# Side work of a Mamba-style scan kernel shared out by what is left of its unit, with the C·h rounds regrouped as three, two, three

## The chip, the cores and the metric

The kernel runs on one core of one Trainium2 chip. The metric is the device time in microseconds (us) of one execution; the median of several runs counts. A TensorE matmul in this kernel is always float32, and the profile records each such matmul as two weight loads and two passes.

## What is computed

The reference takes 2 sequences of 1024 tokens with 512 features (2048 tokens in all), and computes, cut to what matters:

```python
xn    = x * rsqrt(mean(x*x) + 1e-6) * norm_w
xn    = xn * sigmoid((xn @ select_proj_w.T + select_proj_b) * select_gate)
delta, B, C = split(xn @ x_proj_w.T)              # 128 columns each
delta = softplus(delta @ dt_proj_w.T + dt_proj_b) # 512 columns
h     = exp(delta * A) * h + (delta * xn) * B     # per token; state 512 x 128
y     = sum over the 128 states of C * h
x1    = layernorm(x + (y + x * D_param) @ out_proj_w.T)
out   = layernorm(x1 + (silu(x1 @ w_gate.T) * (x1 @ w_up.T)) @ w_down.T)   # 2048 hidden
```

The scan over tokens is the long part: it has 512 x 128 states for each of 2048 tokens.

## The kernel before

**The main loop.** The scan is cut into stretches of 32 tokens (`st`, 64 of them), each into two halves (`i`), and each half into eight *slots*. There are so 1,024 slots, numbered `k`; `r = k % 8` is a slot's *place* in its half. A slot does the same basic work each time: two matmuls for `bu` (L689, the input term), two matmuls for `a` (L407, the exponent of the decay, for the slot after it), both on 32 of the 128 rows of the array; two `Exp` on ScalarE, which read `a` and write `a_sb` (L414); on VectorE a small add that carries the state over (L708) and one scan over 128 x 1024 elements (L709), which reads `a_sb` and `bu` and writes a part of `h`. `bu` has two PSUM buffers, `a` has two (one for each of its matmuls), `a_sb` has three. A matmul for `a` has to wait until ScalarE has read the buffer that it writes.

**C·h.** Eight rounds of four matmuls (`y_round`, L426) for each half multiply `h` of the half before by C. The list `ROUNDS` says which rounds stand at which place. They are issued after the basic work of the slot.

**Side work.** All else is written as Python generators and shared out over the slots at places 0, 2, 3, 5 and 6: the projections of the next lot of 256 tokens (`pre`: units `ss`, `sel`, `xp`, `b`, `z`, `uT`, `t`), the output projection of a tile of 128 tokens (`post`: `zT`, `op`), and the feed-forward part (`ffn`: `x1T`, eight units `gu` and two units `d` for each tile). A *unit* is a group of matmuls into the one PSUM bank that all the side work shares (`ps_m`, one buffer). A generator yields "P" before a unit, "H" between the *parts* of a unit, and "E" at its end; `Work.tensor()` issues one part of the unit that holds the bank, or begins the next unit. A part is one matmul for `d`, `op`, `sel`, `xp` and `ss`, two matmuls for `gu`, and two transposes for `zT`, `x1T` and `uT`. So `gu` has 8 parts (16 matmuls), `d` has 16 parts (16 matmuls), `op` has 8, `sel` and `xp` have 4. `give_back()` at the start of a slot frees the bank of a unit that has ended; what follows it on the other engines (a copy from PSUM, an add) is issued then.

**How many parts a slot gets.** `PARTS` gives a number for each place, and a credit carries over what could not be used:

```python
credit = min(credit + PARTS[r], 6)
for _ in range(min(credit, 4) if PARTS[r] else 0):
    if not work.tensor():
        break
    credit -= 1
```

**Order.** All engines run their instructions in the order in which Python issues them; nothing reorders them later. Weights of `ffn` come in pieces of 512 KB through five buffers, issued on SyncE's queue (L506), some pieces ahead of their use.

**The end.** After the last slot come the last eight rounds of C·h, then whatever side work is left: always the last tile's `zT`, `op`, first layernorm, `x1T`, `gu`, `d` and last layernorm, and what remains of the tile before it (tile 14 of 0 to 15).

Of the kernel before, what the change touches and what calls it, by code (L numbers as in the profile page):

```python
# [17 lines left out]
TC = 256  # L18


ROUNDS = ((), (0, 1, 2), (), (), (3, 4, 5), (), (), (6, 7))
PARTS = (4, 0, 3, 3, 0, 3, 3, 0)
RMS_EPS = 1e-6
LN_EPS = 1e-5

# [9 lines left out]
def kernel(  # L35
# [25 lines left out]
    NF = wgu_s.shape[0]  # L61
    NM = D // P
# [79 lines left out]
    def col(group, m):  # L142
        return vec[:, group, m : m + 1]
# [10 lines left out]

    made = {}

    def misc(name):
        return bank_pool[0].tile([P, 512], FP, tag="m", name=name)


# [3 lines left out]
    def pre(c):  # L164

        t0, n = lots[c]
        n_j, n_s = n // P, n // S
# [15 lines left out]
        def matmuls(ps, w, m, rhs):  # L183
            for k in range(NM):
                nc.tensor.matmul(  # L185
                    ps[:, 0:n], w[:, k, ts(m, P)], rhs[:, k, :],
                    start=(k == 0), stop=(k == NM - 1),
                )
                yield "H" if k + 1 < NM else "E"
# [7 lines left out]
        for m in range(NM):  # L197
            nc.scalar.activation(xT[:, m, :], xT[:, m, :], AF.Copy, scale=col(V_NORM, m))
        yield "P"
        ps = misc(f"ss_{c}")  # L200
        for k in range(NM):
            nc.tensor.matmul(  # L202
                ps[:, 0:n], ones, u[:, k, :], start=(k == 0), stop=(k == NM - 1)
# [12 lines left out]


        for m in range(NM):
            ps = misc(f"sel_{c}_{m}")
            yield from matmuls(ps, sel_w, m, xn)  # L220
            nc.scalar.activation(
                u[:, m, :], ps[:, 0:n], AF.Relu,
                bias=neg[:, 1, m : m + 1], scale=neg[:, 0, m : m + 1],
            )
            nc.scalar.activation(
                dt[:, m, :], ps[:, 0:n], AF.Abs, bias=gate_b[:, m : m + 1], scale=col(V_GATE, m)
            )
            yield "P" if m + 1 < NM else "E"
# [9 lines left out]
            decay()  # L238

        for g, dst in ((0, low), (2, c_sb)):  # L240
            ps = misc(f"xp_{c}_{g}")
            yield from matmuls(ps, xp_w, g, xn)
            nc.scalar.copy(dst, ps[:, 0:n])
            yield "P"

        ps = misc(f"b_{c}")
        for j in range(n_j):
            for k in range(NM):
                nc.tensor.matmul(  # L249
# [12 lines left out]
        yield "P"  # L262

        for a in range(0, NM, 2):
            ps = misc(f"z_{c}_{a}")
            for m in (a, a + 1):
                nc.tensor.matmul(  # L267
                    ps[:, ts(m - a, n)], dt_w[:, ts(m, P)], low, start=True, stop=True
                )
                yield "H" if m == a else "E"  # L270
            for m in (a, a + 1):
                z = ps[:, ts(m - a, n)]
                nc.scalar.activation(u[:, m, :], z, AF.Relu, bias=col(V_DTB, m))
                nc.scalar.activation(dt[:, m, :], z, AF.Abs, bias=col(V_DTB, m))  # L274
            yield "P" if a == 0 else "E"
# [4 lines left out]

        for j in range(n_j):
            yield "P"
            ps = misc(f"uT_{c}_{j}")
            for m in range(NM):
                nc.tensor.transpose(ps[:, ts(m, P)], u[:, m, ts(j, P)], ident)
                if m == 1:
                    yield "H"
            yield "E"
            t = pre_pool.tile([P, D], FP, tag="row", name=f"uT_{c}_{j}")
            nc.scalar.copy(  # L290
                t.rearrange("p (g m c) -> p m g c", g=4, m=NM),
                ps.rearrange("p (m g c) -> p m g c", m=NM, g=4),
            )
            for st in range(4):
                nc.sync.dma_start(
                    ub_d[t0 // S + 4 * j + st, :, :, 0, :].rearrange("g t q -> t g q"),
                    t[ts(st, S), :].rearrange("t (g q) -> t g q", g=4),
                )
            if c == 0:
                load(0)  # L300
                diag(0, 0)
                diag(0, 1)
        yield "P"
        ps = misc(f"t0_{c}")
        for m in range(NM):
            nc.tensor.matmul(
                ps[0:n_s, ts(m, P)],
# [89 lines left out]
    def place(k):  # L397
        h, r = divmod(k, 8)
        m, pair = divmod(r, 2)
        return h, m, pair  # L400
# [47 lines left out]
    def post(tt):  # L448

        zT = post_pool.tile([P, NM, P], FP, tag="zT", name=f"zT_{tt}")  # L450
        nc.sync.dma_start(zT, x_q.rearrange("(m p) t -> p m t", p=P)[:, :, ts(tt, P)])
        yield "E"
        yield "E"
        nc.gpsimd.tensor_tensor(zT, zT, dq.unsqueeze(2).to_broadcast([P, NM, P]), ALU.mult)
        yield "E"
        yield "P"
        ps = misc(f"zT_{tt}")
        for s in range(4):
            nc.tensor.transpose(ps[:, ts(s, P)], yrs[tt][:, s, :], ident)
            if s == 1:  # L460
                yield "H"
        yield "E"
        z = zT.rearrange("p m (s t) -> p s m t", t=S)
        nc.vector.tensor_tensor(
            z, z, ps.rearrange("p (s m t) -> p s m t", m=NM, t=S), ALU.add
        )
        x1 = post_pool.tile([P, D], FP, tag="x1", name=f"x1_{tt}", bufs=4)
        nc.sync.dma_start(x1, xf[tt])
        yield "P"
        ps = misc(f"op_{tt}")  # L470
        for half in (slice(0, 256), slice(256, 512)):
            for k in range(NM):
                nc.tensor.matmul(  # L473
                    ps[:, half], zT[:, k, :], out_w[:, k, half], start=(k == 0), stop=(k == NM - 1)
                )
                yield "H" if half.start == 0 or k + 1 < NM else "E"
        nc.vector.tensor_tensor(x1, x1, ps, ALU.add)
        yield "E"
        yield from normalize(x1, f"a{tt}")
        work.add(ffn(tt, x1))  # L480
# [12 lines left out]
    def ffn(tt, row):  # L493
# [17 lines left out]
        fetch(4)  # L511
        x1T = ffn_pool.tile([P, NM, P], FP, tag="x1T", name=f"x1T_{tt}")
        yield "P"
        ps = misc(f"x1T_{tt}")
        for m in range(NM):
            nc.tensor.transpose(ps[:, ts(m, P)], row[:, ts(m, P)], ident)
            if m == 1:
# [6 lines left out]
        for f in range(0, NF, 2):  # L524
            fetch(at + 4)
            yield "P"
            ps = misc(f"gu_{tt}_{f}")
            for b in range(2):
                w = pieces[at + b].rearrange("p (a k h) -> p a k h", a=2, k=NM)
                for a in range(2):  # L530
                    for k in range(NM):
                        nc.tensor.matmul(  # L532
                            ps[:, ts(2 * a + b, P)], w[:, a, k, :], x1T[:, k, :],
                            start=(k == 0), stop=(k == NM - 1),
                        )
                        if k % 2:
                            yield "E" if a and b and k + 1 == NM else "H"
            at += 2
            gu = ffn_pool.tile([P, 2, 2 * P], FP, tag="gu", name=f"gu_{tt}_{f}", bufs=2)
            nc.scalar.copy(gu, ps.rearrange("p (a t) -> p a t", a=2))  # L540
            work.add(silu(gu, hid[:, f : f + 2, :], f"{tt}_{f}", ready), front=True)
        while len(ready) < NF // 2:
            yield "E"
        for half in range(2):
            fetch(at + 4)
            yield "P"
            ps = misc(f"d_{tt}_{half}")
            for f in range(NF):
                if f == NH:
                    fetch(at + 6)  # L550
                w = pieces[at + f // 4].rearrange("p (f d) -> p f d", f=4)
                nc.tensor.matmul(  # L552
                    ps[:, 0:HD], hid[:, f, :], w[:, f % 4, :],
                    start=(f == 0), stop=(f == NF - 1),
                )
                yield "H" if f + 1 < NF else "E"
            part_of = row[:, ts(half, HD)]
            nc.vector.tensor_tensor(part_of, part_of, ps[:, 0:HD], ALU.add)
            at += 4
# [38 lines left out]
    class Work:  # L598


        def __init__(self):
            self.gens, self.holder = [], None

        def add(self, gen, front=False):
            item = [gen, next(gen)]
# [23 lines left out]
        def tensor(self):  # L629

            if self.holder is not None:
                if self.holder[1] != "H":
                    return False
                self.step(self.holder)
                return True
            for item in self.gens:
                if item[1] == "P":
                    self.holder = item
                    self.step(item)
                    return True  # L640
            return False

# [5 lines left out]
    work = Work()  # L648
# [13 lines left out]
    for b in range(2):  # L662
        decay_exp(0, b, decay_mm(0, b))

    pres, begun, credit = {}, set(), 0
    for k in range(NG):
        h, m, pair = place(k)
        st, i = divmod(h, 2)
        r = k % 8

        if PARTS[r]:
            work.give_back()
        if r == 0:
            hs[h] = half_pool.tile([P, 256, S], FP, tag="h", name=f"h_{h}")
            if i == 0:
                c = lot_of[st]
# [10 lines left out]
        for b in range(2):  # L687
            g = 2 * pair + b
# [26 lines left out]
        if h:  # L715
            for b in ROUNDS[r]:
                y_round(h - 1, b)
        credit = min(credit + PARTS[r], 6)
        for _ in range(min(credit, 4) if PARTS[r] else 0):
            if not work.tensor():  # L720
                break
            credit -= 1

        j, r4 = divmod(k, 4)
        if r4 == 3:
# [93 lines left out]
```

## Time and profile before

| | |
|---|---|
| median of three runs | 2837.61 us (2833.27 to 2842.39) |
| the profiled execution's own time | 2842.96 us |
| its span, first to last instruction | 2841.2 us |
| first scan begins, last scan ends | 43.2 us, 2760.6 us |
| TensorE busy | 2727.4 us (96%) |
| VectorE busy | 2522.9 us (89%) |
| ScalarE, GpSimd busy | 1549.8 us (55%), 1783.3 us (63%) |
| mean granted TensorE clock | 0.987 |

The profiled execution lies 5.4 us above the median of the runs, and its span is 1.8 us shorter than its own time. A line such as `L689 PE MATMUL bu<-du,ub` in the profile means: the instruction of line 689 of the kernel, on TensorE, that reads `du` and `ub` and writes `bu`. In a timeline the first number is the start in us from the start of the span, the second the duration; `[0.86 <-DVE h L709]` says that the engine sat idle for 0.86 us just before and what ended that. A busy TensorE there is an engine with some matmul under way, not one at its peak rate.

### The profile page before, as it was taken

What the parts mean: (1) busy time and instruction counts of PE and PEld (TensorE: products, weight loads), DVE (VectorE), ACT (ScalarE), POOL (GpSimd) and SP (SyncE); (2) the same over time, 40 slices, a digit from 0 to 9 for tenths busy, and PEclk for the clock granted to TensorE, in tenths of its full rate; (3) what the DMA queues carried; (4) which work ended last, traced back from release to release, by engine and by line L of the source; (5) the groups of instructions that cost most, each with busy time, mean ns of one, the idle gap of its engine ahead of it and who ended that gap; (6) DMA issues with size and microseconds to landing.
All of it is one profiled execution on the core that took longest, in us unless ns stands there. A gap on an engine that the chain in (4) does not pass through costs nothing.

```text
span 2841.2 us, 57463 instructions
## 1 busy us (share of the span) xinstructions
PE 2727.4 (96%) x22728; PEld 1484.1 (52%) x22728; DVE 2522.9 (89%) x2144; ACT 1549.8 (55%) x3105; POOL 1783.3 (63%) x2016
## 2 busy tenths in 40 slices
PE   7879999999999999999999999999999999999998
PEld 4324554555555554555544555555555555555558
DVE  2999898999999999999999999999999999999980
ACT  4546555555565455654656556555555554555442
POOL 4556675666667675775667667667576666657552
PEclk7999999999999999999999999999999999999999
DMA  2012222224223232233312333132331323332336
GB/s 75 16 30 66 86 77 79 87 73 134 86 62 116 86 121 64 83 96 105 123 43 84 105 104 104 57 100 93 112 101 47 113 87 109 101 105 96 107 103 208
DMA packets 112380, 258.67 MB, mean 91 GB/s; under 512 B 11568, under 2 KB 49456, under 8 KB 112112
## 3 DMA queue, kind: packets, MB, share of 16 engines
q1 hardware_dynamic: 112112, 254.99, 27.6%
q8 instruction: 181, 2.97, 0.4%
q14 instruction: 87, 0.71, 0.1%
HBM read 242.23 MB, written 12.71 MB: 90 GB/s over the span
## 4 chain that ended last, share of the span: by engine, by line
PE 75%; DVE 18%; issue 3%; ACT 2%; POOL 1%; DMA 0%; SPq 0%; DVEq 0%; POOLq 0%; ACTq 0%
PE bu L689 28%; PE gu L532 17%; DVE h L709 15%; PE y L426 13%; PE d L552 7%; PE a L407 4%; PE sel L185 2%; PE op L473 1%; PE xp L185 1%; DVE bu L708 1%; ACT a_sb L414 1%; PE b L249 1%; PE ss L202 0%; PE z L267 0%; DMA ub_d<-uT 0%
## 5 line engine op out<-in xcount | busy, mean ns | idle before, releaser
L709 DVE TENSOR_TENSOR_SCAN h<-a_sb,bu 128x1024 f32<-128x1024 f32 x1024 | 2341.2, 2287 | 159.2 <-POOL ddt L378 43.2
L414 ACT ACTIVATE a_sb<-a 128x496 f32<-128x496 f32 x2048 | 1089.0, 585 | 1142.6 <-PE a L407 1013.3
L689 PE MATMUL bu<-du,ub 32*128 32x512 f32 x4096 | 1198.0, 646 | 52.5 <-DVE h L709 28.3
L407 PE MATMUL a<-ddt,a_t 32*128 32x512 f32 x4096 | 1240.7, 646 | 2.8 <-ACT t L313 2.8
L378 POOL TENSOR_TENSOR ddt<-dt,hot 128x512 f32<-128x512 f32 x512 | 534.5, 1050 | 225.2 <-PE a L407 225.1
L532 PEld LDWEIGHTS gu<-x1T,w 128*128 128x128 f32 x4096 | 481.7, 192 | 232.8 <-issue 155.0
L388 POOL TENSOR_TENSOR du<-ub,hot 128x512 f32<-128x512 f32 x512 | 536.4, 1052 | 25.7 <-PE a L407 22.3
L532 PE MATMUL gu<-x1T,w 128*128 128x128 f32 x4096 | 537.3, 283 | 11.2 <-ACT t L313 4.5
L689 PEld LDWEIGHTS bu<-du,ub 32*128 32x128 f32 x4096 | 337.2, 184 | 375.8 <-issue 205.6
L426 PE MATMUL y<-h,cz 128*32 128x256 f32 x8192 | 524.7, 385 | 1.9 <-DVE h L709 1.3
L426 PEld LDWEIGHTS y<-h,cz 128*32 128x32 f32 x8192 | 227.7, 109 | 406.7 <-issue 271.9
L407 PEld LDWEIGHTS a<-ddt,a_t 32*128 32x128 f32 x4096 | 371.5, 184 | 19.9 <-ACT a_sb L414 9.6
L708 DVE TENSOR_TENSOR bu<-bu,cd 128x32 f32<-128x32 f32 x992 | 184.9, 186 | 83.1 <-PE a L407 80.2
L552 PE MATMUL d<-w,hid 128*128 128x256 f32 x1024 | 256.9, 393 | 1.1 <-ACT dt L274 1.1
L552 PEld LDWEIGHTS d<-w,hid 128*128 128x128 f32 x1024 | 183.5, 189 | 121.6 <-issue 92.5
L570 POOL TENSOR_SCALAR gu<-gu 128x256 f32<-128x256 f32 x128 | 108.3, 846 | 209.4 <-ACT gu L540 208.4
L578 POOL TENSOR_TENSOR hid<-gu,e 128x256 f32<-128x256 f32 x128 | 93.1, 728 | 141.7 <-ACT e L576 140.8
L440 POOL TENSOR_TENSOR yc<-yc,pick 128x512 f32<-128x512 f32 x64 | 66.7, 1042 | 168.7 <-ACT yc L439 168.7
L365 POOL TENSOR_TENSOR cd<-cd,h 128x256 f32<-128x256 f32 x124 | 106.5, 859 | 44.5 <-DVE h L709 44.5
L571 POOL TENSOR_TENSOR gu<-gu 128x256 f32<-128x256 f32 x128 | 93.4, 730 | 10.7
L540 ACT COPY gu<-gu 128x512 f32<-128x512 f32 x128 | 75.3, 588 | 33.5 <-PE gu L532 33.3
L323 POOL TENSOR_TENSOR dt<-dt,u 128x512 f32<-128x512 f32 (+1 forms) x36 | 41.3, 1151 | 68.7 <-ACT dt L320 68.7
(86 smaller groups left out, 1252.6 us busy)
## 6 DMA issues: line engine op xcount, KB each, us to landing
w<-in_wgu_s_dram SPq DMA_DIRECT2D x256, 512.0 KB, 3.8
w<-in_wd_s_dram SPq DMA_DIRECT2D x128, 512.0 KB, 4.0
cd<-dt_d SPq DMA_DIRECT2D x62, 256.0 KB, 4.0
ub<-ub_d SPq DMA_DIRECT2D x64, 128.0 KB, 2.0
ub_d<-bt SPq DMA_DIRECT2D x64, 64.0 KB, 1.8
ub_d<-uT SPq DMA_DIRECT2D x64, 64.0 KB, 1.8
zT<-in_x_q_dram SPq DMA_DIRECT2D x16, 256.0 KB, 4.0
x<-in_x_dram SPq DMA_DIRECT2D x16, 256.0 KB, 3.6
```

The source lines that it names most:

```text
L365: nc.gpsimd.tensor_tensor(cd, cd, last, ALU.mult)
L378: nc.gpsimd.tensor_tensor(ddts[j][:, m, :, :], made[lot_of[st]][0][:, a + m, toks(st)].unsqueeze(1).to_broadcast([P, 16, S]), hot[:, ts(i, ...
L388: nc.gpsimd.tensor_tensor(dus[j][:, m, :, :], uv[:, a + m, :].unsqueeze(2).to_broadcast([P, 16, S]), hot.unsqueeze(1).to_broadcast([P, 16, ...
L407: nc.tensor.matmul(ps, a_t[ts(g, 32), m, :], ddts[k // 4][ts(g, 32), m % 2, :, :], start=True, stop=True,)
L414: nc.scalar.activation(a_sb[:, k % 3, ts(b, 16), 1:], ps[:, :, 1:], AF.Exp, scale=-1.0)
L426: nc.tensor.matmul(ys[st][ts(m, 32), ts(i, 256)], cz[st % 3][:, at : at + 32], hs[h][:, ts(m, 64), ts(b, 4)], start=(i == 0 and b == 0), s ...
L532: nc.tensor.matmul(ps[:, ts(2 * a + b, P)], w[:, a, k, :], x1T[:, k, :], start=(k == 0), stop=(k == NM - 1),)
L552: nc.tensor.matmul(ps[:, 0:HD], hid[:, f, :], w[:, f % 4, :], start=(f == 0), stop=(f == NF - 1),)
L570: nc.gpsimd.tensor_scalar_max(g, g, -80.0)
L689: nc.tensor.matmul(bu[:, ts(b, 16), :], prepared[st][ts(g, 32), 1, :], dus[k // 4][ts(g, 32), m % 2, :, :], start=True, stop=True,)
L708: nc.vector.tensor_tensor(first, first, left[:, at : at + 2, i, :], ALU.add)
L709: nc.vector.tensor_tensor_scan(hs[h][:, ts(r, 32), :].rearrange("p q t -> p (q t)"), a_sb[:, k % 3, :, :].rearrange("p q t -> p (q t)"), b ...
```

## The change

The rounds of C·h are regrouped: rounds 0 to 2 stay at place 1, rounds 3 and 4 stay at place 4, and rounds 5 to 7 stand at place 7 (before: 3, 4, 5 at place 4 and 6, 7 at place 7). The credit is dropped. Each unit says how many parts it has when it takes the bank (`misc(name, parts)`), and `Work` counts down what is left of it. A slot first issues one part. If three or fewer are left of that unit then, it issues all of them. If more are left, it issues up to as many in all as `PARTS` says, or four if the unit has just begun and the place is 0 or 6. `PARTS` becomes 3, 4, 4, 3, 3 at places 0, 2, 3, 5, 6 (before 4, 3, 3, 3, 3).

```diff
-ROUNDS = ((), (0, 1, 2), (), (), (3, 4, 5), (), (), (6, 7))
-PARTS = (4, 0, 3, 3, 0, 3, 3, 0)
+ROUNDS = ((), (0, 1, 2), (), (), (3, 4), (), (), (5, 6, 7))
+PARTS = (3, 0, 4, 4, 0, 3, 3, 0)
...
-    def misc(name):
+    def misc(name, parts):
+        work.left = parts
         return bank_pool[0].tile([P, 512], FP, tag="m", name=name)
...
-            ps = misc(f"gu_{tt}_{f}")
+            ps = misc(f"gu_{tt}_{f}", 2 * NM)
...
-            ps = misc(f"d_{tt}_{half}")
+            ps = misc(f"d_{tt}_{half}", NF)
...
             if self.holder is not None:
                 if self.holder[1] != "H":
                     return False
+                self.left -= 1
+                self.fresh = False
                 self.step(self.holder)
                 return True
             for item in self.gens:
                 if item[1] == "P":
                     self.holder = item
                     self.step(item)
+                    self.left -= 1
+                    self.fresh = True
                     return True
...
-        credit = min(credit + PARTS[r], 6)
-        for _ in range(min(credit, 4) if PARTS[r] else 0):
-            if not work.tensor():
-                break
-            credit -= 1
+        if PARTS[r] and work.tensor():
+            more = work.left
+            if more > 3:
+                more = (4 if work.fresh and r in (0, 6) else PARTS[r]) - 1
+            for _ in range(more):
+                work.tensor()
```

More of the change, by code (lines that the diff above doesn't have):

```diff
@@ L199, in pre @@
         yield "P"
-        ps = misc(f"ss_{c}")
+        ps = misc(f"ss_{c}", NM)
         for k in range(NM):
@@ L218, in pre @@
         for m in range(NM):
-            ps = misc(f"sel_{c}_{m}")
+            ps = misc(f"sel_{c}_{m}", NM)
             yield from matmuls(ps, sel_w, m, xn)
@@ L240, in pre @@
         for g, dst in ((0, low), (2, c_sb)):
-            ps = misc(f"xp_{c}_{g}")
+            ps = misc(f"xp_{c}_{g}", NM)
             yield from matmuls(ps, xp_w, g, xn)
@@ L244, in pre @@
             yield "P"
-        ps = misc(f"b_{c}")
+        ps = misc(f"b_{c}", n_j)
         for j in range(n_j):
@@ L264, in pre @@
         for a in range(0, NM, 2):
-            ps = misc(f"z_{c}_{a}")
+            ps = misc(f"z_{c}_{a}", 2)
             for m in (a, a + 1):
@@ L282, in pre @@
             yield "P"
-            ps = misc(f"uT_{c}_{j}")
+            ps = misc(f"uT_{c}_{j}", 2)
             for m in range(NM):
@@ L303, in pre @@
         yield "P"
-        ps = misc(f"t0_{c}")
+        ps = misc(f"t0_{c}", 1)
         for m in range(NM):
@@ L456, in post @@
         yield "P"
-        ps = misc(f"zT_{tt}")
+        ps = misc(f"zT_{tt}", 2)
         for s in range(4):
@@ L469, in post @@
         yield "P"
-        ps = misc(f"op_{tt}")
+        ps = misc(f"op_{tt}", 2 * NM)
         for half in (slice(0, 256), slice(256, 512)):
@@ L513, in ffn @@
         yield "P"
-        ps = misc(f"x1T_{tt}")
+        ps = misc(f"x1T_{tt}", 2)
         for m in range(NM):
@@ L601, in __init__ @@
         def __init__(self):
-            self.gens, self.holder = [], None
+            self.gens, self.holder, self.left, self.fresh = [], None, 0, False
         def add(self, gen, front=False):
@@ L663 @@
         decay_exp(0, b, decay_mm(0, b))
-    pres, begun, credit = {}, set(), 0
+    pres, begun = {}, set()
     for k in range(NG):
```

## The prediction

> **What bounds the kernel now.** I read the page's busy times and its chain of work first:
>
> ```profile
> span 2841.2 us, 57463 instructions
> PE 2727.4 (96%) x22728; PEld 1484.1 (52%) x22728; DVE 2522.9 (89%) x2144; ACT 1549.8 (55%) x3105; POOL 1783.3 (63%) x2016
> PE 75%; DVE 18%; issue 3%; ACT 2%; POOL 1%; DMA 0%; SPq 0%; DVEq 0%; POOLq 0%; ACTq 0%
> ```
>
> TensorE carries three quarters of the chain, VectorE most of the rest. VectorE's floor is 2.48 us a slot (scan 2.29, carry add and gaps 0.19), 19.86 us for eight slots. Next, the table of busy time by stretch, over eight slots in which all side work is `gu`:
>
> ```profile
> core 0: us, PE busy (x) PEld busy (x) DVE busy (x) ACT busy (x) POOL busy (x), PEclk, DMA share, GB/s
> 1379.20:1400.10 20.90, 20.90 (x196) 12.15 (x192) 19.49 (x17) 12.27 (x25) 14.75 (x18) 1.00 0.38 127
> ```
>
> TensorE fills all of it, VectorE has a microsecond to spare. So TensorE sets the pace, and what counts is its time slot by slot, from the first `bu` of a slot to that of the next. TensorE's timeline gives it (places 5, 6, 7, and an empty place 0):
>
> ```profile
> 2333.27 0.69 PE L689 MATMUL bu<-du,ub 32*128 32x512 f32 x1
> ...
> 2334.34 0.71 PE L532 MATMUL gu<-x1T,w 128*128 128x128 f32 x4
> 2334.98 0.69 PE L689 MATMUL bu<-du,ub 32*128 32x512 f32 x1
> ...
> 2335.58 0.71 PE L407 MATMUL a<-ddt,a_t 32*128 32x512 f32 x2
> ...
> 2336.63 1.07 PE L426 MATMUL y<-h,cz 128*32 128x256 f32 x16
> 2337.63 0.69 PE L689 MATMUL bu<-du,ub 32*128 32x512 f32 x1
> ...
> 2339.64 0.69 PE L689 MATMUL bu<-du,ub 32*128 32x512 f32 x1 [0.86 <-DVE h L709]
> ```
>
> The slot with one part of `gu` takes 1.71 us. The next slot has two rounds of C·h, which elsewhere make 2.07 us (1383.53 to 1385.60), and takes 2.65: its second `a` starts 0.6 us after its first `bu`, since ScalarE still reads the `a` of the slot before. A short slot saves nothing below some 2.3 us. The empty slot at 2337.63 lasts 2.01 although its work is 0.97; there VectorE is the later one.
>
> Reading all 1,023 slots so, at full clock: 12 matmuls of y 2.51, 8 of y 2.07 (0.108 each); 8, 6, 4, 2 matmuls of `gu` 3.05, 2.60, 2.16, 1.71 (0.223 each); 4, 3, 1 of `d`, `op`, `sel` or `xp` 3.00, 2.56, 1.70 (0.432 each); four transposes 1.66; empty 0.97. Any side work thus costs 0.30 beyond its matmuls (3.05 - 8 x 0.223 - 0.97). These sum to 2516 us, the slots took 2717: 201 us are waits. The waits of short slots, read as the excess of the pair of slots, are steady: y8 0.23, gu4 0.13, gu2 0.58, one matmul 0.59, transposes 0.63, an isolated empty slot 1.3 to 1.6.
>
> The end, TensorE's timeline:
>
> ```profile
> 2760.70 3.64 PE L426 MATMUL y<-h,cz 128*32 128x256 f32 x58 [1.26 <-DVE h L709]
> ...
> 2767.31 0.33 PE L459 MATMUL zT<-ident,yr 128*128 128x128 f32 x1 [2.01 <-POOL yr L442]
> 2769.03 5.41 PE L473 MATMUL op<-out_w,zT 128*128 128x256 f32 x16 [1.39 <-DVE zT L464]
> 2774.27 13.98 PE L552 MATMUL d<-w,hid 128*128 128x256 f32 x64
> 2788.09 0.60 PE L516 MATMUL x1T<-ident,x 128*128 128x128 f32 x4
> 2790.74 30.48 PE L532 MATMUL gu<-x1T,w 128*128 128x128 f32 x256 [2.06 <-ACT x1T L520]
> ```
>
> All 32 `d` of tile 14 stand between the last tile's `op` and its `x1T`; the layernorm there needs 3.5 of these 14 us (2774.4 to 2777.9).
>
> **The change part by part.** The order of the changed program on TensorE shows what goes where; it does what it says.
>
> *Work moved into the loop.* 20 `d` and 2 `gu` more, 4 y fewer (they follow the last slot's `bu`, under the last scan: nothing): 20 x 0.432 + 2 x 0.223 - 4 x 0.108 = +8.7.
>
> *Fewer slots with side work.* Empty slots go from 44 to 56: 12 x 0.30 = -3.6. Work of the slots: +5.1.
>
> *Split units.* One-part slots (gu2, or one matmul) fall from 49 to 17. Before: 49 x 0.585 = 28.7 of wait. After: the 17 follow a y8 slot, whose 0.23 is part of their 0.59 ("y8, d1" gave 0.59 in all), so 17 x 0.36 = 6.1. That is -22.6. `gu4` goes from 23 to 43: +2.6. Of the empty slots 34 and 35 lie in the first 100, where VectorE sets the pace and they cost nothing; the later ones go from 10 to 21: 11 x 1.45 = +16.0 (ends 1.3 and 1.6: 14.3 to 17.6). Sum -4.0.
>
> *Rounds of C·h.* Round 5 moves from place 4 to 7. y12 and y8 slots stay as many, so 0. It reads `h` of the half before, done eight slots ago. The copy of y at place 0 comes 0.43 later, 2.5 before the next round needs the bank. The scan of the next half, which overwrites `h`, starts 1.55 after the next `bu`, which stands behind the round. If this cover were gone: at most 0.43 for each of 64 stretches, no end of mine.
>
> *Queues.* A `gu` unit now ends at place 3 and its copy (0.59 on ScalarE) is issued at place 5, ahead of that slot's `Exp`; the next unit starts 1.06 after that slot's `bu`, so it is covered. Weight pieces land in 3.8 us and are asked for a unit ahead, 9.7 us now (2 x 3.05 + 2.3 + 1.3). GpSimd's and VectorE's lists are the same work in slightly other places.
>
> *`op` after `zT`.* Its add sits on VectorE behind a scan, and `op` waits for it: 11.3 us over the run, without the stall of the next item. Afterwards 13 tiles have `zT` at place 6 and `op` at 0, two slots later; the nearest row (3 and 5) waits 0.78: 10.1. So -1 (ends -11 and +5).
>
> *One stall.* At 433.4 the slot with the first `op` lasted 4.6 too long, and the clock fell to half until 442.4; its eight slots lost 5.9. It may stay or go: -2 (0 to -5.9).
>
> Loop: 5.1 - 4.0 - 1 - 2 = -1.9.
>
> *The end.* From the last scan's end (2760.64) `gu` starts after 30.1 us. After: y 3.6; 12 `d` 5.2; then VectorE first does tile 14's add and statistics (0.4 + 0.7 + 0.2) and only then `zT`'s add (0.7), so `op` starts at about 11.1; `op` at full clock 3.5; layernorm 3.5; `x1T` 0.6, copy 0.6, gaps 0.4: 19.7. That is -10.4. Ahead of the last tile's weights SyncE's queue now has tile 14's output, which waits for its layernorm to about 12; the first piece lands at 16, needed at 19.7. TensorE is more idle here, and the clock shows what that can do (next rows). I take 2 us for it (0 to 3.5): -8.5.
>
> Sum -10.4: the profiled 2841.2 becomes 2830.8, and the median, 5.4 below that execution's own time, 2837.6 - 10.4 = 2827.
>
> **The clock.** Table by stretch again, same columns:
>
> ```profile
> 220.60:224.00 3.40, 2.61 (x16) 1.24 (x16) 3.19 (x5) 2.12 (x4) 3.40 (x4) 0.99 0.00 0
> 224.00:227.40 3.40, 3.40 (x24) 0.90 (x20) 3.30 (x3) 1.58 (x3) 3.14 (x3) 0.50 0.01 2
> ...
> 2787.40:2790.80 3.40, 1.34 (x9) 0.95 (x8) 1.30 (x3) 1.08 (x4) 0.27 (x1) 1.00 0.66 231
> 2790.80:2794.20 3.40, 3.40 (x16) 3.40 (x17) 0.00 (x0) 0.63 (x1) 0.00 (x0) 0.50 0.38 104
> ```
>
> The granted clock (before the last two columns) is half in stretches of 3.4 us that follow stretches in which TensorE was busy for 0.98 to 2.61 us of 3.4. Each costs up to 1.7 us of TensorE's time. None of the ten empty slots after the first 100 has one beside it.
>
> The Trainium skill ("TensorE: Matmul & The Clock Gate", Part 1) says that the clock halves after at least one idle window of about 3.4 us. No empty slot is idle that long, so by the rule the loop loses nothing and the sum stays at 2827. The rows show a fall after a window busy for three quarters; their case stands below, at 2849.
>
> **The rivals.** *The clock falls in the new empty slots* (slower). Place: place 5 after a y8 slot, 21 empty slots after the first 100. Price 1.7 each. For it: a y8 slot and an empty one hold some 2 us of work in 4.6, as little as the stretches above. Against: none of ten before. From 6 such falls the gain is gone, from 11 it is a loss over 0.3%; all 21 give 2827 + 36 = 2863, the 13 that recur every 64 slots or so 2827 + 22 = 2849, which I take.
>
> *The waits are not saved and the end is late* (no change). If the excess of short slots was VectorE's and only showed on TensorE, the loop gains nothing of the 4.0 + 1 + 2 and costs +5.1; with two more half-clock stretches in the end and weights 1.5 us late its gain is 5.5. Sum about 0: 2837. For it: 18% of the chain is VectorE. Against: its spare microsecond in eight slots.
>
> *More waits go* (faster): 8 of `op`'s 11 us go, as `zT` and `op` now always stand two slots apart, and the whole stall: loop 5.1 - 4.0 - 8 - 5.9 = -12.8, end -8.5: 2816. Against: the row at 0.78 is also two slots apart.
>
> **How the numbers follow.** The likeliest case, 0.61, gives 2827 with a range of its own of 2819 (the stall gone 3.9, the end without loss by the clock 2, empty slots at 1.3: 1.7) to 2838 (stall 2, end 1.5, empty slots 1.6, `op` 6). About 0.3% (8.5 us) is what a measurement of this kernel can tell from no change: below 2829.1 is faster, above 2846.1 slower. Two thirds of that case are faster (0.41), one third the same (0.20), since its upper ends seldom come together. Clock rival 0.18, slower. No change 0.13. More waits go 0.08, faster. So faster 0.49, same 0.33, slower 0.18. The range reaches down to 2815 and up to the clock rival, 2849.
>
> **What would show it.** Right: slots of `gu` at places 0, 2, 3, 5, 6 at 2.16, 3.05, 3.05, 2.60, 2.60; eight slots of pure `gu` still 20.9; the last scan ends within 8 us of 2760; `gu` of the last tile starts about 20 after it, not 30. Wrong: half-clock stretches between 442 and 2700; a wait of `gu` for DMA; empty slots at over 2.6 us; `op` waiting over 1.5.

## The result, and the profile after

The changed kernel took 2864.32 us (median of 4 runs, 2862.01 to 2870.0), the kernel before, run beside it, 2836.88 us (2833.27 to 2842.39). The ratio is 1.0098, 95% interval 1.0076 to 1.012: slower by 27 us, where 10 us less were predicted. 2864 lies outside the predicted range. The profiled execution of the changed kernel took 2865.05 us, its span is 2863.2 us.

The page of the changed kernel, busy times and chain of waits by engine:

```profile
span 2863.2 us, 57418 instructions
PE 2715.0 (95%) x22728; PEld 1471.6 (51%) x22728; DVE 2525.2 (88%) x2144; ACT 1547.4 (54%) x3105; POOL 1782.6 (62%) x2016
PE 73%; DVE 19%; issue 3%; ACT 2%; DMA 1%; POOL 1%; SPq 1%; DVEq 0%; ACTq 0%; POOLq 0%
```

TensorE is busy for 12 us less in a span that is 22 us longer: no engine is busy for longer by more than 2.3 us (VectorE), more is waited for. Two shares that were 0% in the chain are now 1%: DMA and SyncE's queue.

Where the time lies is read from two numbers. The last scan ends at 2792.5 us (before 2760.6), and what follows it takes 70.7 us (before 80.5). So the end gave 9.8 us and the loop cost 31.8. Read slot by slot as in the prediction, the loop's work is 2521.4 us against 2516.3, +5.1, and its waits are 227.8 us against 200.5, +27.3 (the first slot begins 0.6 us earlier). I split each slot's wait by where it lies: the second `a` late, which waits for ScalarE (before 101.5, after 87.4); the first matmul of the side work late (before 23.2, after **55.5**); the rest, mostly the next `bu` waiting for VectorE (before 75.8, after 84.9). These are -14.1, +32.3 and +9.1.

The view of what TensorE waited for names the +32.3. Its columns are: line, what released it, us in total, times, longest us. First the kernel before, the only rows in which a unit waits for the add that follows a `d` or an `op`:

```profile
PE gu L532 <- DVE x L477: 2.6, 2, 1.3
PE sel L185 <- DVE x L477: 0.3, 1, 0.3
```

The changed kernel, the rows of that kind and the one for `t` (4.5 us in 3 places before):

```profile
PE gu L533 <- ACT t L314: 10.2, 7, 2.9
PE zT L460 <- DVE x L559: 9.5, 12, 1.2
PE sel L186 <- DVE x L478: 6.9, 6, 1.3
PE ss L203 <- DVE x L559: 6.5, 6, 1.2
PE d L553 <- DVE x L478: 5.3, 6, 0.9
PE x1T L517 <- DVE x L559: 3.7, 6, 0.8
PE d L553 <- DVE x L559: 3.5, 3, 1.2
```

Six of these seven lines have the same form: a unit that has just begun waits for a VectorE add, the one that takes the result of `d` (L559) or `op` (L478) out of PSUM. Together they are 35.4 us in 39 places, where the kernel before has 2.9 us in 3. All side work shares one bank, so the next unit can't begin before that add is done. Both engines' timeline at one such place (the last part of a `d` at place 5, `zT` at place 6; other rows are left out):

```profile
594.69 0.70 PE L553 MATMUL d<-w,hid 128*128 128x256 f32 x2
595.32 0.69 PE L695 MATMUL bu<-du,ub 32*128 32x512 f32 x1
595.35 2.29 DVE L715 TENSOR_TENSOR_SCAN h<-a_sb,bu 128x1024 f32<-128x1024 f32 x1
597.55 0.40 DVE L559 TENSOR_TENSOR x<-x,d 128x256 f32<-128x256 f32 x1
598.01 0.66 PE L460 MATMUL zT<-ident,yr 128*128 128x128 f32 x4 [1.18 <-DVE x L559]
```

The `d` was finished at 595.4. Its add takes 0.40 us, but starts at 597.55: it stands behind the scan, which had started 0.04 us before `d` ended. TensorE is idle for 1.18 us, and the slot, whose work is 1.66 us, lasts 3.27 (595.32 to 598.59). The Trainium skill ("TensorE: Matmul & The Clock Gate", Part 1) describes VectorE as a strict first-in-first-out queue; the 2.16 us between the end of `d` and its add agree with that.

In the program's order the kernel before has three places where a unit follows a `d` or an `op` in the very next slot; the changed kernel has 40. Before, every `d` after the first 72 slots (28 of 28) ended at place 0, 3 or 6, and the next slot had C·h alone: the scan and the add ran beside that. With the changed kernel's shares `d` ends at place 5 (23 times) or 2 (6), `op` at 2 (13), and place 6 or 3 follows at once.

The first line of the seven is another hand-off of the same bank. ScalarE's part of the timeline, around the unit `t` at place 5 (the rows of `Exp` are left out):

```profile
1560.34 0.59 ACT L291 COPY uT<-uT 128x512 f32<-128x512 f32 x1 [1.98 <-DMA ub_d<-uT]
1564.10 0.57 ACT L314 COPY t<-t 8x512 f32<-8x512 f32 x1 [2.22 <-DMA ub_d<-uT]
```

The copy that would free the bank waits for a DMA. `uT` and `t` are copied into one SBUF tile (`row`, one buffer), and the DMA of the previous `uT` still reads it. `gu` after `t` then started 1.7 us late here; this happened six times in the changed kernel (7.7 us) and once before (0.7).

Two readings went as predicted. The table by stretch, over eight slots of pure `gu` (columns as in the prediction):

```profile
665.14:686.06 20.92, 20.92 (x196) 12.14 (x193) 19.41 (x17) 12.47 (x26) 15.60 (x19) 1.00 0.17 53
```

20.92 us where 20.90 were measured before: `gu` hands over to `gu` through a ScalarE copy at no cost. And the end, from TensorE's timeline (earlier and later rows are left out):

```profile
2803.58 3.72 PE L474 MATMUL op<-out_w,zT 128*128 128x256 f32 x16 [1.61 <-DVE zT L465]
2810.80 1.11 PE L517 MATMUL x1T<-ident,x 128*128 128x128 f32 x4 [3.50 <-ACT x L490]
2812.59 30.64 PE L533 MATMUL gu<-x1T,w 128*128 128x128 f32 x256 [0.68 <-ACT x1T L521]
```

`op` starts 11.1 us after the last scan (predicted 11.1), `gu` 20.1 (predicted 19.7).

### The profile page after: what moved, and what is told of

The parts are those of the page before. It is cut to its first block, busy times and chain, and to the rows that moved or that the text cites. A ratio compares the mean times of both kernels' runs of the same rounds, so it can differ in the third digit from the quotient of the medians.

```text
span 2863.2 us, 57418 instructions
## 1 busy us (share of the span) xinstructions
PE 2715.0 (95%) x22728; PEld 1471.6 (51%) x22728; DVE 2525.2 (88%) x2144; ACT 1547.4 (54%) x3105; POOL 1782.6 (62%) x2016
## 4 chain that ended last, share of the span: by engine, by line
PE 73%; DVE 19%; issue 3%; ACT 2%; DMA 1%; POOL 1%; SPq 1%; DVEq 0%; ACTq 0%; POOLq 0%
PE bu L695 27%; PE gu L533 18%; DVE h L715 16%; PE y L427 13%; PE d L553 7%; PE a L408 3%; PE sel L186 2%; PE xp L186 1%; DVE bu L714 1%; DMA ub_d<-uT 1%; PE op L474 1%; ACT a_sb L415 1%; PE b L250 1%; SPq L296 1%; PE z L268 1%
## 5 line engine op out<-in xcount | busy, mean ns | idle before, releaser
L533 PE MATMUL gu<-x1T,w 128*128 128x128 f32 x4096 | 535.3, 283 | 13.3 <-ACT t L314 10.2
L695 PEld LDWEIGHTS bu<-du,ub 32*128 32x128 f32 x4096 | 328.6, 184 | 388.8 <-issue 216.5
L353 POOL TENSOR_TENSOR cd<-a_n,cd 128x512 f32<-128x512 f32 x62 | 78.9, 1272 | 0.0
```

The costliest lines, as they stand in the source:

```text
L533: nc.tensor.matmul(ps[:, ts(2 * a + b, P)], w[:, a, k, :], x1T[:, k, :], start=(k == 0), stop=(k == NM - 1),)
L695: nc.tensor.matmul(bu[:, ts(b, 16), :], prepared[st][ts(g, 32), 1, :], dus[k // 4][ts(g, 32), m % 2, :, :], start=True, stop=True,)
```

## The experiments

Each time is the median of its runs; a ratio is to the kernel before, run on the same chip in the same job (medians 2836.43, 2837.9 and 2836.91 us in the three jobs). "Late starts" are the side-work waits that stood at 23.2 us before and 55.5 after.

**1. Which half of the change costs.** The kernel before with the new `ROUNDS` alone, and the changed kernel with the old ones.

```diff
-ROUNDS = ((), (0, 1, 2), (), (), (3, 4, 5), (), (), (6, 7))
+ROUNDS = ((), (0, 1, 2), (), (), (3, 4), (), (), (5, 6, 7))
```

> The kernel before with only the rounds of C·h regrouped (3, 2, 3), credit and parts as they were. Theory (hand-offs): what costs time in the changed kernel is that units d and op, whose PSUM bank is drained by VectorE behind a scan, now end in a slot whose direct successor begins the next unit (40 times against a handful before). This kernel has the hand-offs of the kernel before: 2837, between 2830 and 2844. Rival (grouping): the short slot with two rounds at place 4 instead of 7 is what costs: 2850 to 2864.

> The changed kernel with the rounds of C·h grouped as before (3, 3, 2); the share-out and PARTS stay changed. Theory (hand-offs): the same 40 hand-offs from d and op, at the same places, so 2864, between 2856 and 2872. Rival (grouping): 2837 to 2845.

The regrouping alone: 2844.7 us, ratio 1.0029 (1.0018 to 1.004), 8 us, about the bound of what can be told from no change. That is 0.7 us above the theory's range and 5 below the rival's; its late starts are 26.4 us. The share-out alone: 2863.83 us, 1.0093 (1.0078 to 1.0108), late starts 49.7. The share-out carries the slowdown.

**2. The bank's way out through VectorE.** `d` and `op` are copied out by ScalarE and added on GpSimd, in the changed kernel and, as a control, in the kernel before.

```diff
-            nc.vector.tensor_tensor(part_of, part_of, ps[:, 0:HD], ALU.add)
+            got = post_pool.tile([P, D], FP, tag="got", name=f"gotd_{tt}_{half}")
+            nc.scalar.copy(got[:, 0:HD], ps[:, 0:HD])
+            nc.gpsimd.tensor_tensor(part_of, part_of, got[:, 0:HD], ALU.add)
...
-        nc.vector.tensor_tensor(x1, x1, ps, ALU.add)
+        got = post_pool.tile([P, D], FP, tag="got", name=f"got_{tt}")
+        nc.scalar.copy(got, ps)
+        nc.gpsimd.tensor_tensor(x1, x1, got, ALU.add)
```

> The changed kernel, but d and op are drained from PSUM by a ScalarE copy into SBUF, and GpSimd adds the copy to the row, instead of one VectorE add that reads PSUM. Order on TensorE is unchanged. Theory (hand-offs): the waits at the start of a unit that follows d or op (37.7 us in the changed kernel's trace, 40 places) fall to under 8: 2834, between 2827 and 2845. Rival (starvation): the new empty slots and the falls of the clock cost the time, and what a wait gives back VectorE takes: 2857 or more.

> The kernel before with the same other drain of d and op, as a control. Theory (hand-offs): it has few hand-offs from d and op, so 2836, between 2829 and 2842. If the other drain helps by itself (less work on VectorE), both kernels gain alike: 2815 or less.

The changed kernel fell by 20 us to 2844.19 (1.003, 1.0018 to 1.0042), the kernel before by 5 to 2831.68 (0.9985, 0.9975 to 0.9994). The same place in the changed kernel with this edit, from ScalarE's, GpSimd's and TensorE's timelines:

```profile
589.56 0.38 PE L555 MATMUL d<-w,hid 128*128 128x256 f32 x1
590.09 0.38 ACT L562 COPY gotd<-d 128x256 f32<-128x256 f32 x1
590.54 0.72 POOL L563 TENSOR_TENSOR x<-x,gotd 128x256 f32<-128x256 f32 x1 [2.82 <-ACT gotd L562]
591.30 0.66 PE L460 MATMUL zT<-ident,yr 128*128 128x128 f32 x4
```

The bank is free at 590.47, before `zT` wants it, and `zT` waits for nothing. The slot lasts 2.37 us in place of 3.27. Late starts fell from 55.5 to 18.3 us, and none of the six `DVE x` lines is left. In the control the same edit is worth 5 us, so about 15 of the 20 belong to the hand-offs.

**3. The copy that waits for a DMA.** Two `row` buffers in the changed kernel.

```diff
-            t = pre_pool.tile([P, D], FP, tag="row", name=f"uT_{c}_{j}")
+            t = pre_pool.tile([P, D], FP, tag="row", bufs=2, name=f"uT_{c}_{j}")
...
-        t = pre_pool.tile([P, D], FP, tag="row", name=f"t0_{c}")
+        t = pre_pool.tile([P, D], FP, tag="row", bufs=2, name=f"t0_{c}")
```

> The changed kernel with two buffers instead of one for the SBUF row into which uT and t are drained. Theory: the 11 us of waits behind uT and t in its trace are the same kind of hand-off, only that there ScalarE's copy waits for the DMA that still reads the one row buffer: 2854, between 2849 and 2858. Rival: the copies themselves take the time, or these waits are covered: 2861 or more.

2852.74 us, 1.0049 (1.0036 to 1.0062), 11.6 us less than the changed kernel. All six `gu` slots after `t` last 3.05 us, where they had lasted 3.88 to 4.76.

**4. Both repairs together.** To make room for both, the kernels below also keep the pool of small tiles at one buffer, `cz` 284 columns wide in place of 288, and the two epsilons in one tile; what that costs by itself was not measured. First the changed kernel:

> The changed kernel with both repairs together: d and op leave PSUM by a ScalarE copy and are added on GpSimd, and the row tile has two buffers. Alone they gave 2844.2 and 2852.7 against 2864.3. Theory (two separate hand-offs of the one bank, each paid by itself): the gains add up, 20.1 + 11.6, less 0 to 3 of common ground: 2833 to 2836, side-start waits 8 to 12 us where the changed kernel has 55.5. It still lies 6 to 10 above the kernel before with the same two repairs (2826.2), by the empty slots near the end of the loop. Rival (both repairs move the same time, the rest is the clock or the empty slots): it stays at 2841 to 2845.

and the kernel before with the same edits:

> The kernel before with the drain of d and op by ScalarE and GpSimd and two row buffers; a candidate for the best. Its waits behind uT and t were some 4 us in the trace: 2828, between 2823 and 2833. If the row buffer matters only where the units stand back to back as in the changed kernel: 2831.

The changed kernel comes to 2831.22 us, 0.9974 (0.9965 to 0.9983), late starts 8.2 us. The two gains of 20.1 and 11.6 add up: 33.1 us, 1.4 more than their sum and 1.8 us below the expected range. The rival, that both edits move the same time, is out. None of the six `DVE x` lines is left in what TensorE waits for, and `gu` waits for `t` once, 0.8 us.

The kernel before with both comes to **2826.17 us**, 0.9955 (0.994 to 0.9969), faster than both kernels. So the repairs bring 12 us there and 33 in the changed kernel: 21 of the 27 us of slowdown are these two hand-offs.

The other 6 us (5 between these two medians) are not a clear loss: one of the ten runs of the changed kernel with both repairs took 2823.71 us, less than every run of the other (2825.98 to 2828.24). In the two profiled executions (2830.6 and 2824.8) the first 72 slots took 188.6 us against 179.5 with the same work (124.2 and 124.5); the changed one ran the stretch from 29.6 on for 41.0 us at half clock, the other 20.5. That stretch differs from kernel to kernel without order (179.5 to 188.6 us over the twelve kernels of this study, at 124.2 to 124.5 of work). From slot 72 on, the changed kernel has 5.4 us more work, 1.4 less waits and an end that is 8.5 shorter: 4.5 us less. What the first stretch's clock depends on stays open.

**5. Other shares for `d`.** Sixteen parts as 4, 4, 4, 4 leave no remainder of one, and every `d` and `op` but one is followed by a slot of C·h again. Tried in the changed kernel alone and with both repairs.

```diff
-        work.left = parts
+        work.left = work.size = parts
...
-                more = (4 if work.fresh and r in (0, 6) else PARTS[r]) - 1
+                more = (4 if work.size == NF or work.fresh and r in (0, 6) else PARTS[r]) - 1
```

> The changed kernel, but a slot always gets four parts of a unit d, so its 16 parts end as 4, 4, 4, 4 and no single one is left over for place 5. In the program's order the hand-offs from d or op into the very next slot fall from 40 to none, zT to op in the next slot rises to 7, and the empty slots after the first 100 rise from 21 to 31. Theory (hand-offs): 37.7 us of waits and 6 of one-part slots go, 7 x 1.3 and 10 x 1.4 come: 2864 - 21 = 2843, between 2836 and 2850. Rival (starvation: empty slots and the falling clock): 2864 or more.

> The changed kernel with the drain of d and op by ScalarE and GpSimd, d in fours and two row buffers together. Theory (hand-offs): what is left against the kernel before with the same drain is the empty slots, less the shorter end: 2834, between 2827 and 2841. Rival (starvation): 2844 or more, as more empty slots cost what the rest gives.

Both missed, and the rival, starvation, came true in both: 2882.79 us (1.0149, 1.0124 to 1.0173) and 2868.65 (1.0109, 1.0086 to 1.0131), 18 and 37 us above the same kernels without the edit. Late starts did fall in the first, to 34.3. But after slot 100 there are 31 empty slots in place of 21, `op` follows `zT` in the next slot 7 times (11.5 us), and the clock falls. The table by stretch of the first of the two:

```profile
1109.60:1113.00 3.40, 2.16 (x9) 0.98 (x10) 3.30 (x4) 1.60 (x3) 3.30 (x5) 1.00 0.00 0
1113.00:1116.40 3.40, 3.40 (x18) 1.13 (x20) 2.15 (x3) 1.32 (x3) 3.40 (x4) 0.50 0.50 154
1116.40:1119.80 3.40, 3.40 (x18) 1.13 (x11) 1.30 (x3) 0.57 (x2) 1.21 (x2) 0.50 0.03 5
```

Between 442 and 2700 us this kernel has 61.4 us at half clock in 12 stretches, the one with both repairs 44.4 in 8; the changed kernel has 6.8 in 2, the kernel before none. At half clock 61.4 us cost up to 30.7, 27.3 more than 6.8 do; the loss is 18 us although late starts gave back 21, so the clock is at most 27 of these 39 us, and the rest was not told apart. Of the 12 stretches eight begin in an empty slot or at most two slots behind one (in five `zT` stands between). The other four have no empty slot beside them: in three `op` stands directly behind `zT` and waits for VectorE, in one `gu` stands directly behind `t`. So empty slots are one place where the clock falls, not the only one; none was isolated. The Trainium skill's rule in the prediction ("TensorE: Matmul & The Clock Gate", Part 1: the clock halves after an idle window of some 3.4 us) does not cover this fall: TensorE was busy for 2.16 us of the 3.40 us before it.

**6. Fewer empty slots.** The changed kernel with both repairs and smaller shares.

```diff
-PARTS = (3, 0, 4, 4, 0, 3, 3, 0)
+PARTS = (3, 0, 4, 3, 0, 3, 3, 0)
```

> The same as the run beside it, with PARTS of 3, 4, 3, 3, 3 at places 0, 2, 3, 5, 6 in place of 3, 4, 4, 3, 3. Empty slots after the first 100 fall from 21 to 6 and one-matmul slots from 17 to none; the work in the loop is 4.4 us more; zT and op stand next to each other 13 times at place 6. Theory (an empty slot costs what VectorE is late in it, 23.1 us for 21 in the trace with the drain repaired, and a one-matmul slot 0.23): 15 x 1.1 = -16.5, -3.9, +4.4 and 13 x 1.1 = +14 for op behind zT: 2 below the run beside it (2826 to 2836). Rival (VectorE's lateness is not the empty slot's own and shows elsewhere once it is gone): +14 or so above the run beside it.

2832.25 us, 0.9976 (0.9962 to 0.999), 1.0 above the run beside it: as the theory had it, and not the rival's 14. But its terms were each too small. The waits for VectorE fell by 29.0 us (88.0 to 59.0; 16.5 + 3.9 expected), and the late starts rose by 24.8 (8.2 to 33.0), of which `op` behind `zT` 19.8 (14 expected). What TensorE waits for has it in one line, where the run beside it has 2.5 us once, in the end:

```profile
PE op L474 <- DVE zT L465: 21.5, 14, 2.5
```

Again a VectorE instruction behind a scan stands between two units in neighbouring slots. Nor do the falls of the clock go with the empty slots: with six of them after slot 100 this kernel has 17.1 us at half clock in five stretches between 442 and 2700 us, the run beside it, with 21, has 10.2 in two (a difference worth up to 3.4 us). Four of the five begin where `op` waits directly behind `zT`.

## Why the prediction was wrong

**Work of the slots: right.** +5.1 predicted, +5.1 counted (2516.3 to 2521.4).

**Split units: direction right, size off.** The two terms, -22.6 and +2.6, are mostly lateness of the second `a`; that fell by 14.1, not 20.0. In the slots behind those with two rounds of C·h, where the 17 one-part slots now stand, it rose from 18.6 to 23.3 us after slot 100.

**Empty slots: right.** The ten before lost 6.7 us after slot 100, the 21 afterwards 24.4: +17.7, predicted +16.0. All waits of the last kind, the stall included, rose by 9.1, where 16.0 - 2 were predicted. The stall at 433 us is gone: the changed kernel has no half-clock stretch there.

**Rounds of C·h at 0: within what can be told.** Alone 0.29% slower (0.18% to 0.4%), at the bound of 0.3%, and beside the share-out without effect (2863.83 against 2864.32). What the 8 us alone come from stays open.

**Queues: the step that failed.** "GpSimd's and VectorE's lists are the same work in slightly other places" counted the instructions that move and not who waits for them. I checked the hand-over from `gu`, whose copy is ScalarE's, and took the bank to be free for the next unit whatever had used it. The place of `d`'s add behind a scan was known from the end and from `op` after `zT`, both costed in the prediction, and not applied to the 40 neighbouring pairs, 3 before. They were put at nothing and cost 37.7 us of late starts (the count in experiment 2's expectation). Experiments 2 and 4 show it: in 2 the gain is 15 us more than in the control, and no unit behind a `d` or an `op` starts late. The profile before had the price: up to 1.3 us at each of the three places where a unit followed at once. The wait for the `row` tile, in the same step, was not costed at all, although the profile before has ScalarE's copy of `t` waiting 9.6 us in 5 places for the DMA of `uT`; with the row edit the changed kernel gains 11.6 us, and the kernel before, already with the other repair, 5.5.

**`op` after `zT`: too small.** -1 predicted. In the neighbouring slots of `zT` and `op` before, 8.0 us of late starts; after, none. The rival "more waits go" had this part right (8 of 11), and the new hand-offs, +40 us, buried it: -8.0 + 40.3 = +32.3.

**The end: right.** -8.5 predicted, -9.8 measured, with 6.8 us at half clock as allowed for.

**The sum.** Loop predicted -1.9, measured +31.8. Of the 34 us between them 33 are late starts (-1 against +32.3); the split units (+5.9) and the last kind of waits (-4.9) nearly cancel.

**The rivals.** The clock rival ended on the right side for a wrong reason: the changed kernel has two half-clock stretches between 442 and 2700, at 2505.8 and 2673.0, worth 3.4 us at most, not 13 to 21. Falls next to empty slots come in experiment 5, eight of its 12. "The waits are not saved" is refuted too: those of `a` did fall. The case that came true, a bank that passes from unit to unit through a busy engine, wasn't on the list.

## What to carry to other kernels

When a change moves where a unit of work ends, list for each shared buffer who clears it, what stands ahead of that instruction on its engine, and who takes the buffer next: the price of a hand-off is what is left then of the instruction in front of the clearing one, and of the clearing one itself. Here, behind a scan of 2.29 us, 39 of the 40 units started 0.3 to 1.4 us late, and in the kernel before a slot without side work between the two units hid the add. A schedule that wastes slots may be hiding such hand-offs. Let an engine that gets to it sooner clear the buffer (here ScalarE), give a tile that a DMA still reads a second buffer, and only then pack the units closer; here these two repairs (with the small edits that make room for them), without closer packing, gave the lowest median of all kernels tried.

## What the runs showed of the hardware

TensorE's clock can fall although TensorE is never idle for long: in experiment 5 it fell to half after a window of 3.40 us with 2.16 us busy, its longest idle time 1.03 us, and then stayed there for 6.8 us in which TensorE counts as busy throughout. The number of empty slots after slot 100 doesn't tell how often: between 442 and 2700 us there were 2 such stretches with 21 of them (the changed kernel), 12 with 31 (experiment 5), but 5 with 6 (experiment 6). Three of the 12 and four of the 5 begin where `op` waits directly behind the short transposes of `zT`.
